# Four graph-attention layers on one core: exponentials and row forms in one pool of six buffers, an 18th weight buffer, and copies of G issued ahead of evictions

## Chip, cores and metric

The kernel runs on one core of a Trainium2 chip. The metric is the device time of one execution in microseconds (us); the kernel before takes 2480.03 us, the median of 3 runs (2478.59 to 2482.91).

The core's engines are named as in the profile: PE multiplies matrices (PEld is its loading of weights, which overlaps), ACT applies functions and copies, DVE and POOL do elementwise work, SP issues most of the transfers (DMA). Each engine runs its instructions in the order in which the program issues them; engines wait for each other by semaphores.

## What is computed

Input `x` holds 16 graphs of 1,024 nodes with 256 features, `adj` one 1,024 x 1,024 adjacency matrix for all. Four attention layers follow each other. Each takes the layer norm of x, then a relu, and adds the attention's result to x. Layers 0 and 2 have 4 heads of 64 features, layers 1 and 3 one head of 256. Cut to one head, a layer is

```python
h = jnp.maximum(_layernorm(x, axis=-1), 0.0)
Wh = jnp.matmul(h, W)
e = leaky(Wh @ a[:D] [:, None] + Wh @ a[D:] [None, :])   # slope 0.2, layer 3: 0.01
alpha = softmax(jnp.where(adj > 0, e, -inf), axis=-1)
x = x + elu(jnp.matmul(alpha, Wh))                       # layer 3: relu
```

## The kernel before

**Steps.** A step is one layer of one graph: 64 steps. Four graphs are in work at a time, and `order_of_steps` interleaves their layers so that from step 8 to step 58 even steps are one-head and odd steps four-head. Each pair of steps takes the same course.

**Preparation of a step** works on two halves of four chunks of 128 nodes. DVE takes the statistics of x (L240), POOL combines them to a shift and a factor (L267 to L279), ACT normalises (L285) into a form called `xn`, ACT splits its 32-bit words into 16-bit halves, `bits` (L294), a DMA transposes these into `turned` (L296), and ACT merges them into the transposed rows `hT` (L302). xn, bits, turned and hT all come from one pool of buffers by the name "rows", HBUFS = 5 of 4 KB a partition. PE projects hT with the layer's matrix, 8 chunks of 2 matmuls (L327); ACT evicts each chunk (L329). From the projection follow, for every node, exponential factors: `rcol` for the sources; those for the targets go through DRAM (L345 to L355) and come back as G, one row of 1,024 values on all partitions, fetched by DMA into `gs` (L371).

**Weights.** For each head ACT copies gs into PSUM (`broadcast`, L383, two buffers: this is "a copy of G"). DVE then makes the head's eight weight tiles, one instruction each (`weights`, L388): max(g, rcol) * mask, 128 x 1,024 values in a buffer of the pool "w", WBUFS = 17. A buffer is free again when the group of matmuls that reads the head's last rows is done.

**Aggregation.** PE multiplies weight tiles with the projected features (L404), and ACT evicts the sums to `y` (L419). A step has eight groups: in a one-head step one block of 128 rows each, so all eight read the same eight tiles; in a four-head step half of a head's rows, so that two groups use up a head.

**Finish.** The step before is finished in pieces during the next step: DVE takes reciprocals (L440), POOL scales y (L450), and for layers 0 to 2 the elu follows: min(y, 0) into a tile `e` (L447 to L452), its exponential on ACT (L456), the sum on DVE (L462), the addition to x on POOL (L463). Layer 3 has a relu and the addition in one DVE instruction (L465). The `e` tiles have two buffers of their own, 4 KB a partition each.

**The order of the instructions** is written out by the loop at the end (L608 to L628). For every group it issues: weight tiles that this group needs and that are still missing; the group's matmuls and its eviction; pieces of the finish that are due; copies of G for the heads that come next (`emit_heads`, L517 to L525); the preparation's pieces due at this group (tables FOUR, ONE and so on, in groups from the step two before); and further weight tiles up to `upto`, the least of six (four-head) or three (one-head) more than issued and of the freed buffers plus WBUFS. `emit_heads(i)` copies a head if its first tile's place is at most

```python
min(i + C // 2, done["tiles"] + C, len(tiles) - 1)        # L519, C = 8
```

and only if its step is prepared. The same function is called by `emit_tiles` (L527) ahead of each tile.

**Weight columns.** The projection matrices of layers 1 to 3 get extra columns, W times the attention vectors, in pieces at fixed groups: the vectors are loaded (L139 on) into a tile of the name "e", spread over the partitions by a matmul (L149), multiplied on DVE into the columns, and bounds for the exponents are taken.

Of the kernel before, what the change touches and what calls it, by code (L numbers as in the profile page):

```python
# [26 lines left out]
F32 = mybir.dt.float32  # L27
# [9 lines left out]
P = 128  # L37
EPS = 1e-5
SHIFT = 60.0
STREAMS = 4  # L40
WBUFS = 17
HBUFS = 5

# [22 lines left out]
def kernel(ctx: ExitStack, tc: tile.TileContext, x, adj, ws, avs, out):  # L68
    nc = tc.nc
    B, N, F = x.shape  # L70
    C = N // P
    K = F // P
    HALF = C // 2
# [26 lines left out]
    prep = ctx.enter_context(tc.tile_pool(name="prep", bufs=2))  # L100
    small = ctx.enter_context(tc.tile_pool(name="small", bufs=4))
    work = ctx.enter_context(tc.tile_pool(name="work", bufs=2))
# [30 lines left out]
    def weight_columns(l):  # L133

        H, slope, hs, _ = LAYERS[l]
        D = F // H
        st = {}

        def vectors(queue=nc.sync):  # L139

            st["a"] = prep.tile([P, HALF, H, D], F32, name="e")
            queue.dma_start(
                out=st["a"][0:1, 2:4],
                in_=bass.AP(tensor=avs[l].tensor, offset=avs[l].offset,
                            ap=[[0, 1], [D, 2], [hs, H], [1, D]]))

        def spread():
            pa = bank(2, H, D)
            nc.tensor.matmul(pa.rearrange("p t h d -> p (t h d)"), lhsT=ones[0:1, :],  # L149
                             rhs=st["a"][0:1, 2:4].rearrange("p t h d -> p (t h d)"),  # L150
                             start=True, stop=True)
            nc.scalar.activation(st["a"][:, 0:2], pa, AF.Copy)

        def columns(ks=range(K)):
            for k in ks:
                for part in range(2):
                    prod = st["a"][:, 2 + part]
                    wk = heads_of(wx[l], H)[:, k]
                    nc.vector.tensor_mul(prod, wk[:, :, 0:D], st["a"][:, part])
                    nc.vector.tensor_reduce(  # L160
                        wk[:, :, D] if part else wx[l][:, k, F + H:F + 2 * H], prod, AX.X, ALU.add)
            if K - 1 not in ks:
                return
            st["sq"] = small.tile([P, K, H], F32, name="sq", bufs=1)
            wd = heads_of(wx[l], H)[:, :, :, D]
            nc.vector.tensor_tensor(st["sq"], wd, wd, op=ALU.mult)

        def bound():

            pn = bank(H)  # L170
            for k in range(K):
                nc.tensor.matmul(pn, lhsT=ones, rhs=st["sq"][:, k, :], start=(k == 0),
                                 stop=(k == K - 1))
            top = small.tile([P, 1], F32, name="top", bufs=1)
            nc.vector.tensor_reduce(top, pn, AX.X, ALU.max)
            nc.gpsimd.tensor_tensor(top, top, half1, op=ALU.pow)
            nc.gpsimd.tensor_scalar(cbias[l], top, 16.01, None, op0=ALU.mult)
            nc.gpsimd.tensor_scalar(nbias[l], top, -16.01 * slope, None, op0=ALU.mult)
            nc.gpsimd.tensor_scalar(rbias[l], top, -16.01 * (1.0 - slope), SHIFT,
                                    op0=ALU.mult, op1=ALU.add)  # L180

        return vectors, spread, columns, bound

    pairs = {}
# [240 lines left out]
    def finish(n):  # L425

        b, l = steps[n]
        H = LAYERS[l][0]
        D = F // H
        st = state[n]  # L430

        def views(half):
            s = slice(half * HALF, (half + 1) * HALF)
            return (xs[b][:, s, :].rearrange("p c (h d) -> p (c h) d", h=H),
                    st["y"][:, s, :, 0:D].rearrange("p c h d -> p (c h) d"),
                    st["r"][:, s, :].rearrange("p c h -> p (c h)"))

        def divide():
            st["r"] = small.tile([P, C, H], F32, name="r")
            nc.vector.reciprocal(st["r"], st["y"][:, :, :, D])  # L440

        def scaled(half):
            xh, yh, r = views(half)
            rb = r[:, :, None].to_broadcast([P, HALF * H, D])
            if l < L - 1:

                e = st["e", half] = prep.tile([P, HALF * H, D], F32, name="e")  # L447
                if H > 1 and slack(n):
                    nc.vector.scalar_tensor_tensor(e, yh, 0.0, rb, op0=ALU.min, op1=ALU.mult)  # L449
            nc.gpsimd.tensor_tensor(yh, yh, rb, op=ALU.mult)  # L450
            if l < L - 1 and not (H > 1 and slack(n)):
                nc.gpsimd.tensor_scalar(e, yh, 0.0, -3.0e38, op0=ALU.min, op1=ALU.max)  # L452

        def exponential(half):
            if l < L - 1:
                nc.scalar.activation(st["e", half], st["e", half], AF.Exp)  # L456

        def add(half):
            xh, yh, r = views(half)
            if l < L - 1:  # L460
                e = st["e", half]
                nc.vector.scalar_tensor_tensor(e, e, -1.0, yh, op0=ALU.add, op1=ALU.max)  # L462
                nc.gpsimd.tensor_add(xh, xh, e)  # L463
                return
            nc.vector.scalar_tensor_tensor(xh, yh, 0.0, xh, op0=ALU.max, op1=ALU.add)  # L465

        def store(half):
            nc.sync.dma_start(
                out=out[b].rearrange("(p c) f -> p c f", p=P)[:, half * HALF:(half + 1) * HALF],
                in_=xs[b][:, half * HALF:(half + 1) * HALF, :])  # L470
            if half == 1 and b + STREAMS < B:
                load(b + STREAMS)


        at = (0, 0, 0, 0, 1, 1, 1) if slack(n) and H > 1 else (0, 0, 1, 1, 2, 2, 3)
        return list(zip(at, (divide, lambda: scaled(0), lambda: scaled(1), lambda: exponential(0),
                             lambda: exponential(1), lambda: add(0), lambda: add(1)))) + (
                    [(4, lambda: store(0)), (4, lambda: store(1))] if l == L - 1 else [])
# [38 lines left out]
    def emit_heads(i):  # L517

        while done["g"] <= min(i + C // 2, done["tiles"] + C, len(tiles) - 1):  # L519
            n, h, _ = tiles[done["g"]]  # L520
            if n >= done["prepared"]:
                break
            broadcast(n, h)
            done["g"] += C
            fetch_heads()  # L525
# [13 lines left out]
    for n, (b, l) in enumerate(steps):  # L539

        free = -99
        if b % STREAMS in last:
            over = last[b % STREAMS] + 1
            free = 8 * over + (8 if l == 0 else 2 if LAYERS[steps[over][1]][0] == 1 else 4)
        last[b % STREAMS] = n
        start = 8 * (n - 2)
        kind = ONE if LAYERS[l][0] == 1 else SOON if n < 5 else FOUR
        if kind is FOUR and free > start + kind[0]:
            kind = SHORT
        if kind is ONE and free > start + kind[0]:  # L550
            kind = TIGHT
        if free > start + kind[0]:
            kind = LATE
            start = max(free, agenda_of[-1][0] + 5, start - LATE[7])
        agenda_of.append([start + k for k in kind] if n > 1 else FIRST)
        if n > 2:

            assert agenda_of[n][7] >= 8 * (n - 2)
            assert agenda_of[n][3] >= agenda_of[n - 1][12]
    ending = []  # L560
    later = {}
    with tc.manual_schedule():
# [40 lines left out]
            load_weights(i)  # L603

        for l, at in ((1, 1), (2, 8 * 3 + 3), (3, 8 * 5 + 3)):
            for i, piece in zip((0, 1, 2, 8), layer[l]):
                later[at + i] = piece
        for n in range(len(steps)):  # L608
            for k, (h, i0, per) in enumerate(groups(n)):
                while planned < len(steps) and min(  # L610
                        a[0] for a in agenda_of[planned:planned + 2]) <= 8 * n + k:
                    plan(planned)
                    planned += 1
                emit_tiles(place[n, h, C - 1] + 1, must=True)
                aggregate(n, h, i0, per)
                if i0 + per == C:
                    done["free"] = place[n, h, C - 1] + 1
                while ending and ending[0][0] <= k:
                    ending.pop(0)[1]()
                upto = min(done["tiles"] + (6 if per > 1 else 3), done["free"] + WBUFS)  # L620
                emit_heads(upto - 1)
                if 8 * n + k in later:
                    later[8 * n + k]()
                prepare(8 * n + k)
                emit_tiles(upto)
            for _, piece in ending:
                piece()
            ending = finish(n) if n < len(steps) - 1 else []  # L628
# [35 lines left out]
```

## Time and profile before

| | before |
|---|---|
| time, median of 3 | 2480.03 us |
| span of the profiled execution | 2479.7 us |
| PE busy | 2403.9 us |
| DVE busy | 2044.1 us |
| ACT busy | 1482.8 us |
| POOL busy | 1071.2 us |
| weight tiles (L388), 1,280 | 1540.8 us, 1274 ns each |
| copies of G (L383), 159 | 162.7 us, 1023 ns each |
| splits (L294), 124 | 236.2 us, 1905 ns each |
| merges (L302), 124 | 265.7 us, 2143 ns each |

The profile is of one execution. A line of the time line has the start, the length, the engine, the line of the kernel, the operation, its output and inputs by the program's names, and in brackets how long the engine was idle before it and what it waited for. In lists of waits the three numbers are the total in us, the number of waits and the longest. The ends of matmuls are modelled.

### The profile page before, as it was taken

The numbers are of one execution on the slowest core, as the hardware profiler recorded it, in microseconds if no ns is written. First come the engines' busy times: TensorE is split into PE (matmuls) and PEld (weight loads), VectorE is DVE, ScalarE is ACT, GpSimd is POOL, SyncE is SP. The second block draws the span as 40 slices with busy tenths as digits, with TensorE's granted clock in tenths as the row PEclk, the third lists the DMA queues.
The fourth block names the chain that finished last, engine by engine and source line by source line (L and its number), as shares of the span: only waits on it lengthen the run. The fifth ranks groups of instructions, "written<-read, shape, count | busy, mean of one in ns | idle before, by whom it ended". The sixth has DMA issues, their size and how long they took to land.

```text
span 2479.7 us, 86492 instructions
## 1 busy us (share of the span) xinstructions
PE 2403.9 (97%) x39104; PEld 2158.6 (87%) x39104; DVE 2044.1 (82%) x2138; ACT 1482.8 (60%) x2501; POOL 1071.2 (43%) x1366
## 2 busy tenths in 40 slices
PE   7899999999999999999999999999999999999989
PEld 5788898898898888888889888889888898888878
DVE  8997677888888988888888888888888888887963
ACT  5465666556665556755556765656655566666451
POOL 3235455443344444544433554543444444554341
PEclk9999999999999999999999999999999999999999
DMA  4322232333433322323433322223334322323221
GB/s 179 80 54 61 44 79 53 78 96 79 112 72 93 79 55 52 79 62 103 109 91 88 79 62 70 70 55 94 95 76 106 104 55 61 79 56 75 72 52 60
DMA packets 294760, 193.39 MB, mean 78 GB/s; under 512 B 264182, under 2 KB 266998, under 8 KB 292472
## 3 DMA queue, kind: packets, MB, share of 16 engines
q1 hardware_dynamic: 294382, 187.86, 30.5%
q8 instruction: 306, 5.01, 0.8%
q14 instruction: 62, 0.51, 0.1%
q10 hardware_dynamic: 10, 0.00, 0.0%
HBM read 105.39 MB, written 17.43 MB: 50 GB/s over the span
## 4 chain that ended last, share of the span: by engine, by line
PE 86%; DVE 6%; DMA 3%; ACT 3%; issue 2%; POOL 1%; DVEq 0%; SPq 0%; ACTq 0%; POOLq 0%
PE bank L404 68%; PE bank L327 17%; DVE w L388 4%; DMA rows<-rows 3%; ACT rows L302 1%; DVE bn L240 1%; ACT rows L285 0%; DVE e L462 0%; ACT rows L294 0%; POOL rstd L273 0%; DVE mask L213 0%; POOL x L463 0%; DMA x<-in_x 0%; PE bank L351 0%; DVE wx L160 0%
## 5 line engine op out<-in xcount | busy, mean ns | idle before, releaser
L404 PE MATMUL bank<-whx,w 128*64 128x65 f32 x36864 | 1909.4, 241 | 40.1 <-DVE w L388 27.5
L404 PEld LDWEIGHTS bank<-whx,w 128*64 128x64 f32 x36864 | 1755.3, 145 | 200.6 <-DVE w L388 33.8
L388 DVE SCALAR_TENSOR_TENSOR w<-g,rcol,mask 128x1024 f32<-128x1024 f32 x1280 | 1540.8, 1274 | 232.6 <-PE bank L404 135.9
L339 POOL TENSOR_TENSOR whx<-whx 128x1024 f32<-128x1024 f32 x128 | 243.4, 1902 | 858.8 <-ACT whx L337 858.8
L419 ACT ACTIVATE y<-bank 128x260 f32<-128x260 f32 (+1 forms) x504 | 191.9, 384 | 658.1 <-PE bank L404 657.8
L327 PE MATMUL bank<-wx,rows 128*128 128x264 f32 (+1 forms) x2048 | 487.3, 392 | 14.5 <-ACT rows L302 7.5
L327 PEld LDWEIGHTS bank<-wx,rows 128*128 128x128 f32 x2048 | 383.6, 192 | 89.4 <-ACT rows L302 15.5
L450 POOL TENSOR_TENSOR y<-y,r 128x1024 f32<-128x1024 f32 x126 | 260.7, 2078 | 233.8 <-DVE e L449 180.5
L463 POOL TENSOR_TENSOR x<-x,e 128x1024 f32<-128x1024 f32 x96 | 227.1, 2365 | 179.8 <-DVE e L462 179.8
L285 ACT ACTIVATE rows<-x,shift,rstd 128x256 f32<-128x256 f32 x512 | 264.6, 589 | 65.6 <-POOL shift L279 64.0
L329 ACT ACTIVATE whx<-bank 128x264 f32<-128x264 f32 (+1 forms) x512 | 189.4, 385 | 170.3 <-PE bank L327 169.9
L302 ACT ACTIVATE rows<-rows 128x2048 uint16<-128x2048 uint16 x124 | 265.7, 2143 | 21.1 <-DMA rows<-rows 21.1
L294 ACT ACTIVATE rows<-rows 128x2048 uint16<-128x2048 uint16 x124 | 236.2, 1905 | 2.2
L462 DVE SCALAR_TENSOR_TENSOR e<-e,y 128x1024 f32<-128x1024 f32 x96 | 190.9, 1989 | 50.1 <-ACT e L456 41.5
L240 DVE BATCH_NORM_STATS2 bn<-x 128x6 f32<-128x256 f32 x512 | 175.5, 410 | 33.2 <-POOL x L463 30.0
L383 ACT ACTIVATE g<-gs 128x1024 f32<-128x1024 f32 x159 | 162.7, 1023 | 27.1 <-DVE w L388 15.1
L273 POOL TENSOR_TENSOR rstd<-rstd,neghalf 128x4 f32<-128x4 f32 (+1 forms) x97 | 120.2, 1239 | 15.0 <-DVE shift L274 7.6
L456 ACT ACTIVATE e<-e 128x1024 f32<-128x1024 f32 x96 | 100.8, 1050 | 1.0 <-POOL e L452 1.0
L440 DVE RECIPROCAL r<-y 128x32 f32<-128x32 f32 (+1 forms) x63 | 17.3, 275 | 82.9 <-ACT y L419 82.8
L449 DVE SCALAR_TENSOR_TENSOR e<-y,r 128x1024 f32<-128x1024 f32 x58 | 68.5, 1222 | 2.1
L465 DVE SCALAR_TENSOR_TENSOR x<-y,x 128x1024 f32<-128x1024 f32 x30 | 36.5, 1218 | 8.9 <-POOL y L450 8.9
L337 ACT ACTIVATE whx<-whx,nbias 128x16 f32<-128x16 f32 (+1 forms) x128 | 40.3, 315 | 4.2
(67 smaller groups left out, 443.6 us busy)
## 6 DMA issues: line engine op xcount, KB each, us to landing
gs<-grow SPq DMA_DIRECT2D x159, 512.0 KB
x<-in_x SPq DMA_DIRECT2D x15, 1024.0 KB
out<-x SPq DMA_DIRECT2D x30, 512.0 KB
w<-in_adj SPq DMA_DIRECT2D x8, 512.0 KB
rows<-rows SPq DMA_TRANSPOSE x124
x<-in_x SPq DMA_DIRECT2D x2, 512.0 KB
wx<-in_L_gnn_W SPq DMA_DIRECT2D x8, 128.0 KB
out<-x SPq DMA_DIRECT2D x8, 128.0 KB
```

The source lines that it names most:

```text
L240: nc.vector.bn_stats(bn[:, c, :], xs[b][:, c, :])
L285: nc.scalar.activation(xn[:, :, q, :], xs[b][:, c, :].rearrange("p (k i) -> p k i", k=K), AF.Relu, bias=st["shift"][:, c:c + 1], scale=st[ ...
L294: nc.scalar.activation(bits, xn.rearrange("p (n s) -> p s n", s=2), AF.Copy)
L302: nc.scalar.activation(st["hT", half].rearrange("p k i -> p (k i)").bitcast(U16).rearrange("p (n s) -> p n s", s=2), st["turned", half].re ...
L327: nc.tensor.matmul(pw, lhsT=st["hT", half][:, k, q * P:(q + 1) * P], rhs=wx[l][:, k, :], start=(k == 0), stop=(k == K - 1))
L339: nc.gpsimd.tensor_tensor(wh[:, :, :, 0:D], wh[:, :, :, 0:D], wh[:, :, :, D:D + 1].to_broadcast([P, HALF, H, D]), op=ALU.mult)
L388: nc.vector.scalar_tensor_tensor(w, state[n]["g", h], state[n]["rcol"][:, jc, h:h + 1], masks[LAYERS[steps[n][1]][3]][:, jc, :], op0=ALU.m ...
L404: nc.tensor.matmul(acc[o % P:o % P + cols, q, :], lhsT=st["w", h, jc][:, o:o + cols], rhs=st["whx"][:, jc, h * (D + 1):(h + 1) * (D + 1)], ...
L419: nc.scalar.activation(st["y"][:, i0:i0 + per, h, :], acc, AF.Copy)
L450: nc.gpsimd.tensor_tensor(yh, yh, rb, op=ALU.mult)
L462: nc.vector.scalar_tensor_tensor(e, e, -1.0, yh, op0=ALU.add, op1=ALU.max)
L463: nc.gpsimd.tensor_add(xh, xh, e)
```

## The change

The change has three parts.

- Buffers. The `e` tiles of the finish come from the pool "rows", which grows from 5 to 6 buffers; the vectors of the weight columns come from the pool "w", which grows from 17 to 18. The two buffers of "e" are gone, so that the memory stays the same.
- The pieces of the weight columns: vectors, then spread and columns together one group later, bounds eight groups after the vectors as before. So the weight buffer that the vectors take is given back sooner.
- Order. The freed buffers and `upto` are worked out ahead of the group's aggregation, and `emit_heads` is called ahead of it too, with C // 2 = 4 more in one-head steps. It is meant to have G ready before DVE wants it, in place of behind the eviction and the pieces of the finish, and a whole head ahead.

```diff
-WBUFS = 17
-HBUFS = 5
+WBUFS = 18
+HBUFS = 6
...
-            st["a"] = prep.tile([P, HALF, H, D], F32, name="e")
+            st["a"] = work.tile([P, HALF, H, D], F32, name="w", bufs=WBUFS)
...
-                e = st["e", half] = prep.tile([P, HALF * H, D], F32, name="e")
+                e = st["e", half] = prep.tile([P, HALF * H, D], F32, name="rows",
+                                                    bufs=HBUFS)
...
-            for i, piece in zip((0, 1, 2, 8), layer[l]):
-                later[at + i] = piece
+            vectors, spread, columns, bound = layer[l]
+            later[at] = vectors
+            later[at + 1] = lambda spread=spread, columns=columns: (spread(), columns())
+            later[at + 8] = bound
...
                 emit_tiles(place[n, h, C - 1] + 1, must=True)
-                aggregate(n, h, i0, per)
                 if i0 + per == C:
                     done["free"] = place[n, h, C - 1] + 1
+                upto = min(done["tiles"] + (6 if per > 1 else 3), done["free"] + WBUFS)
+
+                emit_heads(upto - 1 + (0 if per > 1 else C // 2))
+                aggregate(n, h, i0, per)
                 while ending and ending[0][0] <= k:
                     ending.pop(0)[1]()
-                upto = min(done["tiles"] + (6 if per > 1 else 3), done["free"] + WBUFS)
-                emit_heads(upto - 1)
```

## The prediction

> **What bounds the kernel now.** I began with the busy shares and the chain of work that ended last.
>
> ```profile
> PE 2403.9 (97%) x39104; PEld 2158.6 (87%) x39104; DVE 2044.1 (82%) x2138; ACT 1482.8 (60%) x2501; POOL 1071.2 (43%) x1366
> PE 86%; DVE 6%; DMA 3%; ACT 3%; issue 2%; POOL 1%; DVEq 0%; SPq 0%; ACTq 0%; POOLq 0%
> ```
>
> PE works for 2403.9 of 2479.7 us, so an edit that leaves the matmuls alone can gain at most 75.8 us. The answer by windows says where they lie: PE is idle for 36.8 us before 400, 23.0 us between 400 and 2240 and 16.3 us after. The change touches little of the first and third, so the steady part comes next: the list of waits between 467 and 2260, which are 24 equal pairs of a one-head step (even) and a four-head step (odd), (2260.39 - 467.05) / 24 = 74.7 us each. PE's entries:
>
> ```profile
> PE bank L404 <- issue: 9.3, 9, 1.6
> PE bank L404 <- DVE w L388: 5.3, 24, 0.2
> PE bank L327 <- ACT whx L329: 4.6, 7, 1.2
> PE bank L327 <- issue: 1.1, 2, 0.6
> PE bank L327 <- ACT rows L302: 0.3, 1, 0.3
> ```
>
> Columns are the total, the number, the longest. Only the second is a wait that the change is aimed at: once a pair, 0.22 us, for a weight tile. DVE's own waits for G (L388 <- ACT g L383) are large, 61.2 us in 24, but DVE is not the bound. So I ask not what DVE gains but what the moved copies do to what PE waits for. That needs the time line of ACT in one pair (one-head step 34; columns: start, length, instruction, idle before it and releaser):
>
> ```profile
> 1374.96 0.38 ACT L419 ACTIVATE y<-bank 128x257 f32<-128x257 f32 x1 [2.17 <-PE bank L404]
> 1375.24 1.02 ACT L383 ACTIVATE g<-gs 128x1024 f32<-128x1024 f32 x1
> 1378.09 2.07 ACT L285 ACTIVATE rows<-x,shift,rstd 128x256 f32<-128x256 f32 x4 [1.82 <-POOL shift L279]
> 1380.19 1.91 ACT L294 ACTIVATE rows<-rows 128x2048 uint16<-128x2048 uint16 x1
> 1382.01 0.37 ACT L419 ACTIVATE y<-bank 128x257 f32<-128x257 f32 x1
> 1382.27 2.06 ACT L285 ACTIVATE rows<-x,shift,rstd 128x256 f32<-128x256 f32 x4
> 1384.37 1.91 ACT L294 ACTIVATE rows<-rows 128x2048 uint16<-128x2048 uint16 x1
> 1386.19 0.37 ACT L419 ACTIVATE y<-bank 128x257 f32<-128x257 f32 x1
> 1386.45 2.14 ACT L302 ACTIVATE rows<-rows 128x2048 uint16<-128x2048 uint16 x1
> ```
>
> and PE's beside it:
>
> ```profile
> 1383.67 5.16 PE L404 MATMUL bank<-whx,w 128*128 128x257 f32 x23
> 1388.66 3.51 PE L327 MATMUL bank<-wx,rows 128*128 128x258 f32 x15
> ```
>
> From 1378.09, when POOL's shift releases the first normalisation, to 1388.59, when the first merge (L302) ends, ACT has no gap. The first projection (L327) needs that merge and starts at 1388.66, 0.07 us after it. PE's one-head aggregation, begun at 1364.33 and 24.33 us long, ends at 1388.66 as well. So the merge comes exactly in time, with no slack: whatever is put into this chain of ACT reaches PE in full. The step two earlier shows the same (merge 1312.66 to 1314.79, projection at 1314.87). Twice the trace shows a later merge, once this:
>
> ```profile
> 411.41 2.15 ACT L302 ACTIVATE rows<-rows 128x2048 uint16<-128x2048 uint16 x1 [0.40 <-DMA rows<-rows]
> 413.61 2.67 PE L327 MATMUL bank<-wx,rows 128*128 128x258 f32 x11 [0.43 <-ACT rows L302]
> ```
>
> A merge 0.40 us late cost PE 0.43 us; at 1911.51 one 0.37 us late cost 0.30.
>
> **What the Trainium skill says.** "Perfetto Trace Analysis", in the part on the Tensor Engine's instruction, says that ACT, DVE and GpSimd are strictly first in, first out, and that PE's end times are modelled. The trace agrees on ACT: the eviction at 1386.19 stood behind split and normalisation, though its group had been done some 3.6 us earlier (six groups of 24.33 / 8 = 3.04 us from 1364.33 end at 1382.6). "ScalarE: Activation LUTs", in the part on what ACT_TABLE_LOAD costs, gives an ACTIVATE with immediate scale and bias 186 ns + 0.833 ns a column, 1039 ns for 1,024, and an overlap of about 93 ns with its neighbour. The trace has 1.02 us for a copy of G, and 0.95 us to the next start in a full queue (255.38 to 256.32 is 0.94). I take 0.95 us.
>
> **The change, part by part.**
>
> *Copies of G ahead of evictions, a head ahead.* I followed the loop by hand for the pair above, counting weight tiles. Step 35's tiles begin at place p; at step 34's sixth group (k=5) nine of them have been issued, and the new bound is min(upto - 1 + 4 + 4, tiles + 8) = p + 17, so that head 2's copy (place p + 16) is emitted there, before that group's eviction. In the kernel before, head 2's copy follows the first eviction of step 35 (1396.61). In the ACT queue it now stands between the second split and the eviction at 1386.19, in the middle of the full chain. Behind it: that eviction, the first merge, two more evictions; behind the merge: PE's first projection. Its own inputs are no wait: its PSUM buffer is head 0's, whose eighth tile DVE ends at about 1385.6 (1375.94 + 8 x 1.2), before the split ends at 1386.28. Head 1's copy stays in the gap before 1378.09 (it moves ahead of the eviction at 1374.96, which waits 2.17 us anyway), so it buys the chain nothing. The merge, and with it PE, is 0.95 us later in each pair with an even step from 10 to 56: 24 x 0.95 = +22.8. Step 8 has 0.4 us of slack: +0.55. Steps 3 and 6 have 3.3 and 1.6: nothing.
>
> What it gives: DVE's wait for head 2's copy, 2.51 us before 1397.66, goes. But DVE's next tile waits 4.13 us, until 1403.08, for a weight buffer that PE frees, so the earlier tile only lengthens that wait. Gain on PE: nothing.
>
> *The 18th buffer.* DVE may run one tile further ahead. In the four-head step head 2's eighth tile, now behind the elu at 1410.23 (or L465 for the relu layers), goes ahead of it, and the 0.22 us that PE waits for it at 1412.70 disappears: 25 x 0.22 = -5.5.
>
> *Prologue and tail.* Step 4 stalls 3.46 us at 257.64 because the statistics (L240, 2.7 us) stand before a tile; with another buffer they stand after it: -2.7. The same reordering delays preparation of steps 3 and 4 by a tile (1.2): +1.2. Among the last steps one stall shrinks by a tile, -1.2, and one preparation comes a tile later, +1.2. Together -1.5.
>
> *Columns.* The column vector's tile moves to the pool of weight buffers and its pieces together. It happens three times, and the slot is given back before the first group that would want it: 0, at most 1.2 each.
>
> *The pool of six.* Two exponential tiles and five forms share six buffers. In relu layers no exponential exists, and the sixth buffer is free. In the pairs with an elu one-head layer the second split at 1411.80 finds live: two exponentials (POOL adds them from 1411.54 to 1413.92 and from 1415.08 to 1417.47), first bits, first turned, second rows, and itself: exactly six. So whether anything waits depends on which buffer a tile gets. The compiled kernel before takes the longest free one, not the next in rotation (one merge takes the buffer of four requests ago, the next preparation that of six), so I take no wait: 0. The other end is the split waiting for the POOL add, 2.1 us, in 13 pairs.
>
> Sum: +22.8 + 0.55 - 5.5 - 1.5 = +16.4. From 2480.0: **2496 us**.
>
> **Rivals.**
>
> *The pool waits as well.* If buffers came in strict rotation, the second split would want the first exponential's buffer, and wait from 1411.80 to 1413.92; transpose, merge and second half of the projection follow, and the next first merge would wait for the second exponential. I work out 0.4 to 2.15 us in each of 13 pairs, 1.5 in the mean, 19.5 together: 2515.9. For it: exactly six are live. Against: the buffers of before do not rotate.
>
> *The copy is hidden.* If the order of ACT does not turn out as counted, or the chain moves earlier because POOL's shift does, only the gains stand: 2480.0 - 5.5 - 1.5 = 2473, or 2470 if gaps called issue shrink too. For it: ACT is busy only 60%, and the shift depends on DVE, which has fewer waits. Against: the statistics before the shift wait for POOL (1374.62, 1.16 <- POOL x L463), which the change doesn't speed up, and the chain is full in every pair that I looked at.
>
> *No change.* Half of the delay is absorbed somewhere: 11.7 - 5.5 - 1.5 = +4.7, 2484.7, which can't be told from no change. Nothing in the trace speaks for exactly that.
>
> **How the numbers follow.** Copy in the chain alone 0.60 (0.85 to 1.02 us a copy, columns 0 to 3.6, prologue and tail -2.5 to 0: 2493 to 2503), with pool waits too 0.17 (to 2518), hidden 0.13 (2468 to 2475), in balance 0.10. The range from 2478 to 2518 leaves out the hidden case and the far ends. Faster 0.13, same 0.10, slower 0.77.
>
> **What would show it.** DVE's waits for ACT g L383 should nearly vanish (61.2 us before) and PE's 0.22 us waits for w L388 too. PE or its weight loads should wait about 0.95 us before the first projection of each one-head step for rows L302, some 23 us together, with a G copy between split and merge in ACT's time line; the pair grows to about 75.4 us. A wait of split or merge for POOL x L463 would show the first rival. I am wrong if the first merge still ends with the aggregation: then the chain began earlier, or the copy stands elsewhere.

## The result, and the profile after

The changed kernel takes 2500.3 us (median of 4 runs, 2499.28 to 2502.73): 1.0089 times the kernel before, 95% interval 1.0067 to 1.011. The forecast was 2496. The profiled execution is 2498.4 us long, 18.7 us more than before. Its busy shares and its chain of work that ended last:

```profile
PE 2404.9 (96%) x39104; PEld 2152.7 (86%) x39104; DVE 2043.2 (82%) x2138; ACT 1483.5 (59%) x2501; POOL 1072.8 (43%) x1366
PE 67%; DVE 11%; ACT 10%; DMA 5%; issue 5%; POOL 2%; DVEq 0%; ACTq 0%; POOLq 0%
```

No engine has more work: PE is busy for 2404.9 us, 2403.9 before. But the chain now runs through ACT for 10% of the span, 3% before. The time is idle time of PE, and the list of PE's waits between 467 and 2260 names it (total, number, longest):

```profile
PE bank L327 <- ACT rows L302: 19.3, 24, 0.9
PE bank L404 <- issue: 8.6, 8, 1.7
PE bank L327 <- ACT whx L329: 5.9, 12, 1.6
PE bank L327 <- issue: 0.8, 2, 0.5
PE bank L327 <- ACT y L419: 0.2, 1, 0.2
```

The first line stood at 0.3 us in one wait before; now it comes once in each of the 24 pairs. The wait for a weight tile (L404 <- DVE w L388, 5.3 us before) is gone. The time line of ACT in the one-head step that answers to the one shown of before:

```profile
1382.55 2.07 ACT L285 ACTIVATE rows<-x,shift,rstd 128x256 f32<-128x256 f32 x4 [2.75 <-POOL shift L279]
1384.65 1.91 ACT L294 ACTIVATE rows<-rows 128x2048 uint16<-128x2048 uint16 x1
1386.47 0.37 ACT L419 ACTIVATE y<-bank 128x257 f32<-128x257 f32 x1
1386.74 2.06 ACT L285 ACTIVATE rows<-x,shift,rstd 128x256 f32<-128x256 f32 x4
1388.83 1.91 ACT L294 ACTIVATE rows<-rows 128x2048 uint16<-128x2048 uint16 x1
1390.65 1.01 ACT L383 ACTIVATE g<-gs 128x1024 f32<-128x1024 f32 x1
1391.59 0.37 ACT L419 ACTIVATE y<-bank 128x257 f32<-128x257 f32 x1
1391.86 2.13 ACT L302 ACTIVATE rows<-rows 128x2048 uint16<-128x2048 uint16 x1
```

and PE's:

```profile
1385.73 7.55 PE L404 MATMUL bank<-whx,w 128*128 128x257 f32 x34
1394.04 3.75 PE L327 MATMUL bank<-wx,rows 128*128 128x258 f32 x16 [0.76 <-ACT rows L302]
```

The copy of G (L383) has come to lie between the second split and the sixth eviction, and the merge ends 0.94 us later after the first normalisation than before (11.44 us in place of 10.50). The normalisation itself starts equally late in both kernels: 13.76 us after PE resumes the aggregation behind the transpose of the factors (L351) in the same step (1378.09 - 1364.33; 1382.55 - 1368.79). So nothing made up for the copy. PE's true loss is larger than the 0.76 us in brackets, since that wait is counted from a modelled end of the last matmul. The distance between starts is safer: from that resumption, the first matmul of the step's second group, to the first projection it is 24.39 us in the mean of 24 steps before, and 25.30 us after. This distance, called A below, turned out to be the sharpest reading of all.

DVE no longer waits for G (61.2 us before), but

```profile
DVE w L388 <- PE bank L404: 155.9, 24, 6.6
```

its wait for a freed weight buffer rose from 99.0 to 155.9 us: the sum of both is 160.2 before and 155.9 after.

Three readings locate the 18.7 us: +0.5 up to the first projection of step 12 (491.27 before, 491.79 after), +14.1 in the 23 pairs from there (74.74 to 75.35 us a pair), +4.1 from the last of these projections to the end (269.4 to 273.5 us). The +0.5 is a sum of larger parts; "The start" below takes it apart.

### The profile page after: what moved, and what is told of

It reads as the page before. It is cut to its first block, busy times and chain, and to the rows that moved or that the text cites. A ratio compares the mean times of both kernels' runs of the same rounds, so it can differ in the third digit from the quotient of the medians.

```text
span 2498.4 us, 86573 instructions
## 1 busy us (share of the span) xinstructions
PE 2404.9 (96%) x39104; PEld 2152.7 (86%) x39104; DVE 2043.2 (82%) x2138; ACT 1483.5 (59%) x2501; POOL 1072.8 (43%) x1366
## 4 chain that ended last, share of the span: by engine, by line
PE 67%; DVE 11%; ACT 10%; DMA 5%; issue 5%; POOL 2%; DVEq 0%; ACTq 0%; POOLq 0%
PE bank L404 50%; PE bank L327 17%; DVE w L388 8%; DMA rows<-rows 4%; ACT rows L302 4%; ACT rows L285 2%; DVE rows L463 2%; POOL x L464 1%; DVE bn L240 1%; ACT g L383 1%; ACT y L419 1%; ACT rows L457 1%; PE bank L351 0%; ACT rows L294 0%; POOL rstd L273 0%
## 5 line engine op out<-in xcount | busy, mean ns | idle before, releaser
L404 PE MATMUL bank<-whx,w 128*64 128x65 f32 x36864 | 1902.5, 241 | 32.2 <-DVE w L388 19.3
L404 PEld LDWEIGHTS bank<-whx,w 128*64 128x64 f32 x36864 | 1749.3, 145 | 191.5 <-issue 28.1
L388 DVE SCALAR_TENSOR_TENSOR w<-g,rcol,mask 128x1024 f32<-128x1024 f32 x1280 | 1537.9, 1272 | 215.1 <-PE bank L404 187.1
L419 ACT ACTIVATE y<-bank 128x260 f32<-128x260 f32 (+1 forms) x504 | 189.9, 383 | 598.7 <-PE bank L404 596.7
L329 ACT ACTIVATE whx<-bank 128x264 f32<-128x264 f32 (+1 forms) x512 | 188.9, 386 | 195.8 <-PE bank L327 195.2
L464 POOL TENSOR_TENSOR x<-x,rows 128x1024 f32<-128x1024 f32 x96 | 227.2, 2367 | 179.6 <-DVE rows L463 179.6
L302 ACT ACTIVATE rows<-rows 128x2048 uint16<-128x2048 uint16 x124 | 265.6, 2142 | 20.9 <-DMA rows<-rows 20.8
L463 DVE SCALAR_TENSOR_TENSOR rows<-rows,y 128x1024 f32<-128x1024 f32 x96 | 192.1, 2002 | 45.5 <-ACT rows L457 38.3
L383 ACT ACTIVATE g<-gs 128x1024 f32<-128x1024 f32 x159 | 161.8, 1019 | 47.9 <-DVE w L388 24.7
L457 ACT ACTIVATE rows<-rows 128x1024 f32<-128x1024 f32 x96 | 100.6, 1048 | 0.1
L450 DVE SCALAR_TENSOR_TENSOR rows<-y,r 128x1024 f32<-128x1024 f32 x58 | 70.1, 1251 | 2.1
```

Source lines behind the costliest of these rows:

```text
L302: nc.scalar.activation(st["hT", half].rearrange("p k i -> p (k i)").bitcast(U16).rearrange("p (n s) -> p n s", s=2), st["turned", half].re ...
L388: nc.vector.scalar_tensor_tensor(w, state[n]["g", h], state[n]["rcol"][:, jc, h:h + 1], masks[LAYERS[steps[n][1]][3]][:, jc, :], op0=ALU.m ...
L404: nc.tensor.matmul(acc[o % P:o % P + cols, q, :], lhsT=st["w", h, jc][:, o:o + cols], rhs=st["whx"][:, jc, h * (D + 1):(h + 1) * (D + 1)], ...
L419: nc.scalar.activation(st["y"][:, i0:i0 + per, h, :], acc, AF.Copy)
```

## The experiments

All in one table. A is the distance just named, "pair" the mean of 23 pairs, "end" the stretch from the last of them to the end; these three are from one profile each, and the time is the median, with the ratio to the kernel before and its 95% interval. How far one profile can be trusted shows in e11, whose steady part has the same instructions as the changed kernel's: its pair takes 75.47 us, 75.35 there.

| kernel | us | ratio (interval) | A | pair | end |
|---|---|---|---|---|---|
| before | 2478 to 2482 | | 24.39 | 74.74 | 269.4 |
| changed | 2500.3 | 1.0089 (1.0067 to 1.011) | 25.30 | 75.35 | 273.5 |
| e1 buffers alone | 2481.7 | 1.0 (0.999 to 1.0011) | 24.40 | 74.75 | 269.6 |
| e2 order alone | 2505.1 | 1.0097 (1.008 to 1.0114) | 25.32 | 75.55 | 273.6 |
| e3 copy behind the merge | 2474.5 | 0.9971 (0.9962 to 0.9981) | 24.42 | 74.67 | 269.5 |
| e4 no head further ahead | 2474.2 | 0.9979 (0.9971 to 0.9987) | 24.40 | 74.63 | 270.0 |
| e5 idle copy, sixth group | 2501.5 | 1.0089 (1.0076 to 1.0103) | 25.29 | 75.84 | 268.3 |
| e6 idle copy, fourth group | 2479.1 | 1.0002 (0.9995 to 1.001) | 24.38 | 74.75 | 268.9 |
| e7 e3, split sooner | 2538.9 | 1.0239 (1.0214 to 1.0264) | 24.42 | 77.02 | 271.3 |
| e8 merge ahead of the copy | 2488.1 | 1.0033 (1.0022 to 1.0045) | 24.41 | 74.99 | 273.9 |
| e9 before, no second transpose | 2470.4 | 0.9969 (0.9958 to 0.9981) | 24.41 | 74.50 | 268.5 |
| e10 e1, no second transpose | 2462.5 | 0.9935 (0.9923 to 0.9947) | 24.37 | 74.17 | 267.4 |
| e11 changed, step 58 as e4 | 2499.8 | 1.0069 (1.0046 to 1.0092) | 25.30 | 75.47 | 269.2 |

**The two halves of the change.** e1 keeps the buffers and undoes the order:

```diff
-                emit_heads(upto - 1 + (0 if per > 1 else C // 2))
                 aggregate(n, h, i0, per)
...
+                emit_heads(upto - 1)
```

> The changed kernel with the order of the loop as before: 18 weight buffers, the pool of six and the columns' new places are kept, the copies of G stand behind evictions again. Theory (the copy of head 2 lies in a full stretch of ACT that ends in the merge PE waits for): head 2's copy goes behind the last eviction of the one-head step, the first merge ends with the aggregation again, PE's 24 waits of 0.22 us for a weight tile stay away: 2479.3 - 5.5, with prologue and tail between 2470 and 2478. Rival 1 (the pool of six or the 18th buffer costs the time): about 2495 to 2500, as the changed kernel. Rival 3 (a copy ahead of an eviction costs by holding back the eviction's PSUM bank): 2470 to 2478 as well.

e2 is the kernel before with the new order alone.

> The kernel before with the order of the loop alone: 17 weight buffers, five row forms and two exponentials of their own. Theory: head 2's copy stands between the second split and the first merge as in the changed kernel; PE waits 0.8 us for the merge in 24 pairs and keeps the 0.22 us waits: 2479.3 + 19.4, with a few us of the tail: 2498 to 2506. Rival 1: 2476 to 2482. Rival 3: 2498 to 2506.

The split is clean on the main question: A is 25.32 with the order and 24.40 with the buffers, so in the steady part the pool of six and the 18th buffer cost nothing and the order costs all. But e1's time missed the expectation of the theory. It equals the kernel before, although the 0.22 us waits are gone. PE's waits in e1 between 467 and 2260:

```profile
PE bank L404 <- issue: 12.3, 8, 2.5
PE bank L327 <- ACT whx L329: 10.7, 11, 1.7
PE bank L327 <- issue: 0.7, 1, 0.7
```

Waits for the eviction L329 were 4.6 us before and are 10.7 here. This is taken up again in e7, e9 and e10.

**The place of the copy.** e3 is the changed kernel with head 2's copy one group later, behind the merge:

```diff
-                emit_heads(upto - 1 + (0 if per > 1 else C // 2))
+                emit_heads(upto - 1 + (0 if per > 1 or k == 5 else C // 2))
```

> The changed kernel, but at the sixth group of a one-head step heads are copied no further than upto - 1, so that head 2's copy is issued one group later, behind the first merge and ahead of the seventh group's eviction. Theory: PE's waits for the merge vanish, the 0.22 us waits stay away, 2470 to 2479 (the tail may keep up to 4 us of the change). Rival 1: 2495 to 2500. Rival 3: the seventh eviction is held back as the sixth was; 2490 or more.

e4 leaves out C // 2 altogether; head 2's copy is then issued at the eighth group, still ahead of that eviction.

> The changed kernel without the extra C // 2: copies stand ahead of evictions, but no head further ahead; head 2's copy is issued ahead of the eighth group's eviction, behind the first merge. Theory: 2470 to 2479. Rival 1: 2495 to 2500. Rival 3: 2490 or more, with PE waiting for banks in the first projection.

Both fell inside the theory's expectation. The same copy, with the same buffers, is worth 26 us between its places: 2500.3 between split and merge, 2474.5 just behind the merge. A is back at 24.42 and 24.40. In the profiles (2498.4 and 2472.5 us) 15.8 us of the difference lie in the 23 pairs, 4.0 in the end and 6.1 in the start. e3 and e4 are also below the kernel before, by 0.29% and 0.21%; their pairs are only 0.07 and 0.11 us shorter, no more than the changed kernel and e11 differ, so where this gain lies is not shown.

**A copy that nobody needs.** To separate ACT's time from all that an earlier G could do to DVE, e5 adds to the kernel before

```diff
+                if per == 1 and k == 5 and 10 <= n <= 56:
+                    nc.scalar.activation(idle, masks[0][:, 0, :], AF.Copy)
                 aggregate(n, h, i0, per)
```

> The kernel before with one more copy of 1,024 values on ACT (a mask, 8 bits, into a tile that nobody reads) ahead of the sixth group's eviction in the 24 one-head steps from 10 to 56; no buffer, no order and no dependence is changed. Theory (ACT is full from the first normalisation to the first merge, and PE waits for the merge): about 0.9 us a step, 24 x 0.9 = +21.6, 2497 to 2505. Rival (the loss in the changed kernel comes from DVE starting head 2 sooner, or from its memory traffic): 2478 to 2484.

and e6 the same with `k == 3`.

> The same additional copy two groups sooner, ahead of the fourth group's eviction, where ACT waits for PE and then for POOL's shift. Theory: the gap takes it up, 2478 to 2484. Rival (any further instruction in ACT's queue costs, by the evictions behind it): as much as in the sixth group, about 2500.

e5's time line of ACT (line numbers behind the insertions are moved by one or more; L303 is the merge):

```profile
1393.86 1.91 ACT L295 ACTIVATE rows<-rows 128x2048 uint16<-128x2048 uint16 x1
1395.68 1.04 ACT L617 ACTIVATE idle<-mask 128x1024 uint8<-128x1024 uint8 x1
1396.62 0.37 ACT L420 ACTIVATE y<-bank 128x257 f32<-128x257 f32 x1
1396.89 2.14 ACT L303 ACTIVATE rows<-rows 128x2048 uint16<-128x2048 uint16 x1
```

and its first wait of PE:

```profile
PE bank L328 <- ACT rows L303: 19.3, 24, 0.9
```

The idle copy reproduces the changed kernel's wait to the tenth: 19.3 us in 24, A 25.29. It costs 22.9 us in all, 0.95 us each. (In the profile the pair grew by 1.10 us, 0.90 of it in A; the cause of the other 0.20 is not shown.) Two groups earlier, where ACT waits for PE and then for POOL, the same 1.05 us cost nothing (A 24.38). So it is ACT's time in this stretch, and neither DVE's earlier start nor a buffer.

**The merge ahead of the copy.** e8 keeps the copy a head ahead and moves the merge in front of it by due times:

```diff
-ONE = (2, 2, 2, 3, 4, 3, 5, 7, 7, 7, 7, 4, 7, 8, 8, 8, 8, 8, 11, 11, 12)
+ONE = (2, 2, 2, 3, 3.7, 3, 3.9, 7, 7, 7, 7, 3.8, 7, 8, 8, 8, 8, 8, 11, 11, 12)
```

> The changed kernel with the first merge of the one-head steps issued behind the second split of the same group, so ahead of head 2's copy and of the sixth eviction; the copy stays a whole head ahead and ahead of that eviction. Theory (only the place of the copy before the merge costs): 2470 to 2479. Rival (the copy's place before evictions or its earliness costs): 2490 to 2500.

It came out between the two: A is repaired (24.41), and yet a pair takes 0.32 us more than in e3. PE's time line and the list of its weight loads' waits say why:

```profile
1386.58 4.09 PE L327 MATMUL bank<-wx,rows 128*128 128x258 f32 x16
```

```profile
PEld bank L327 <- ACT y L419: 12.3, 25, 0.7
```

The projection's first half takes 4.09 us in place of 3.75: three evictions now stand behind merge and copy together, and the projection runs out of PSUM buffers until they are done. In e3 that line is 0.2 us in one wait. So the third theory, an eviction held back, was not wrong but small: 0.3 us a pair in e8; in the changed kernel, where that line is 0.7 us in one wait, the wait for the merge comes first and hides it.

**Where the gain of the 18th buffer went.** In e1, PE's waits for L329 lie in four-head steps. One of them is seen from ACT:

```profile
1272.61 2.15 ACT L302 ACTIVATE rows<-rows 128x2048 uint16<-128x2048 uint16 x1 [2.54 <-DMA rows<-rows]
1274.66 1.21 ACT L329 ACTIVATE whx<-bank 128x264 f32<-128x264 f32 x4
```

The second half's merge waits 2.54 us for its transpose, and four evictions of the projection stand behind it. In the same pair of the kernel before the merge did not wait; PE had lost 1.15 us to a gap called issue just before. Over all pairs merges waited 22.3 us for transposes in 18 waits in e1, and 16.1 us in 16 before. e7 tried to bring that transpose forward, by splitting one group sooner:

```diff
-FOUR = (-8, -8, -5, 0, 2, 1, 4, 5, 5, 5, 5, 3, 4.5, 5, 5, 5, 5, 6, 8, 8, 10)
+FOUR = (-8, -8, -5, 0, 2, 1, 4, 5, 5, 5, 5, 2, 4.5, 5, 5, 5, 5, 6, 8, 8, 10)
```

> The kernel with head 2's copy behind the first merge (2474.5), and the second split of the four-head steps due at 2 in place of 3, behind the second normalisation and ahead of that group's eviction and of gT, where ACT was idle 1.4 us. Theory (the gain of the 18th buffer was eaten up because the second merge of the four-head step then waits for its transpose, with evictions of the projection behind it): the transpose is issued about 1.8 us sooner, PE's waits for L329 (7.6 us) go, 2466 to 2471. Rival (what PE loses is gaps called issue, and these take the place of any wait that goes; or the fetch of G, now behind the transpose on SP, comes too late): 2472 to 2480.

A miss by far, 64 us above e3. The transposes did come in time: merges waited for them 0.6 us in one wait, in e3 21.1 us in 20. But the rival that the fetch of G comes too late had the direction, though not the size. SP's queue and ACT's answer in one pair:

```profile
1358.97 2.87 SPq L296 DMA_TRANSPOSE rows<-rows  x1
1361.89 0.47 SPq L355 DMA_DIRECT2D grow<-gT  x1
1363.39 0.33 SPq L371 DMA_DIRECT2D gs<-grow  x1
```

```profile
1367.79 1.03 ACT L383 ACTIVATE g<-gs 128x1024 f32<-128x1024 f32 x1 [2.87 <-DMA gs<-grow]
```

Issuing the transpose holds SP until 1361.84, and only then are the next step's factors, on hand since 1359.37, written and fetched. The fetch is issued 5.1 us after PE's transpose of the factors (L351 at 1358.28), 1.9 us in the pair of the kernel before (1262.24 to 1264.15). The copy of G then waits on ACT with evictions behind it, 95.2 us in 39 such waits (5.4 in 8 before), and PE waits for evictions: 24.0 us for L329 and 22.4 us for L419.

So the wait was taken away in another manner. e9 and e10 leave the second transpose of four-head steps out, from the kernel before and from e1:

```diff
+            if half == 1 and H > 1 and n > 8:
+                st["turned", half] = bits.rearrange("p s (n i) -> p s n i", i=P)
+                return
```

> The kernel before, but in four-head steps from the ninth on the second half's transpose by DMA is left out: the merge reads the split's output itself (so the rows of that half are not turned, and the output is not the reference's; every other instruction stays). Theory (in a pair PE either loses about 1 us to a gap called issue or to the eviction L329 that stands behind a merge waiting for its transpose): the merges of this half no longer wait, PE's waits for L329 (4.6 us) go, the 0.22 us waits for tiles stay: 2472 to 2478. Rival (gaps or other waits take their place): 2478 to 2483.

> The same left out of the kernel with the buffers alone (2481.7), where PE waited 10.7 us for L329. Theory: those waits go, and now the 18th buffer shows its gain: 5 us below the same cut in the kernel before, 2467 to 2473. Rival (the 18th buffer is worth nothing because issue gaps take the place of any wait): the same time as the cut in the kernel before, within 2 us.

PE's waits in e9 and in e10 (L407 is the aggregation, L330 the projection):

```profile
PE bank L407 <- issue: 9.8, 6, 2.1
PE bank L407 <- DVE w L391: 5.3, 24, 0.2
PE bank L330 <- ACT rows L305: 0.7, 1, 0.7
PE bank L330 <- issue: 0.4, 1, 0.4
```

```profile
PE bank L407 <- issue: 10.4, 8, 2.4
PE bank L330 <- issue: 1.0, 1, 1.0
PE bank L330 <- ACT rows L305: 0.4, 1, 0.4
PE bank L330 <- ACT whx L332: 0.2, 1, 0.2
```

Without that transpose the waits for the eviction are gone (0 and 0.2 us), the gaps called issue stay about the same, and the 18th buffer shows its gain: 2470.4 against 2462.5, and 0.33 us a pair. Both are some us lower than expected. With the transpose in place the same buffers gave nothing (e1). Leaving it out also frees SP and DMA engines for everything else, so how much of the drop of both belongs to the merge's wait alone stays open; the difference between the two, which share it, does not depend on that. (e10 also has the pool of six and the new places of the columns; it is the vanished L407 <- DVE w line, 5.3 us, that points to the 18th buffer.)

**The end.** In step 58 the changed kernel's copy was not ready to run:

```profile
2295.58 1.03 ACT L383 ACTIVATE g<-gs 128x1024 f32<-128x1024 f32 x1 [3.58 <-DVE w L388]
2296.54 0.37 ACT L419 ACTIVATE y<-bank 128x257 f32<-128x257 f32 x1
2296.80 2.13 ACT L302 ACTIVATE rows<-rows 128x2048 uint16<-128x2048 uint16 x1
```

```profile
2296.96 1.16 PE L327 MATMUL bank<-wx,rows 128*128 128x264 f32 x4 [1.27 <-ACT y L419]
2299.27 5.07 PE L327 MATMUL bank<-wx,rows 128*128 128x264 f32 x14 [1.15 <-ACT whx L329]
```

Its PSUM buffer was still being read by DVE, so it held ACT for 3.58 us, and the eviction and the merge behind it; PE lost 1.27 + 1.15 us there. e11 takes C // 2 away in step 58 alone.

> The changed kernel, with the extra C // 2 left out in step 58 alone, where head 2's copy waits 3.58 us for DVE to free its PSUM buffer, with an eviction and the second merge behind it. Theory: the steady part stays (75.35 us a pair), the stretch from the last pair's first projection to the end, 273.5 us in the changed kernel and 269.4 before, comes back to 269 to 271; the whole 2500.3 - 4 = 2496. Rival (the end is longer because of what the steady part leaves behind): 273 to 274 and 2500.

The end fell to 269.2 us, as in the kernel before, while A stayed at 25.30. The whole time, 2499.8, does not show these 4 us beyond its interval; its profile is longer elsewhere, by 0.12 us a pair and 1.8 us in the start, where the edit changes nothing. What e11 shows rests on the stretch in its profile. The same 273.6 and 273.9 appear in e2 and e8, the other kernels that issue this copy ahead of the sixth group's eviction.

**The start.** In steps 3 and 6 the changed kernel's copy was not ready either. It stood between the second split and the merge and waited for DVE:

```profile
217.76 1.03 ACT L383 ACTIVATE g<-gs 128x1024 f32<-128x1024 f32 x1 [2.00 <-DVE w L388]
335.63 1.03 ACT L383 ACTIVATE g<-gs 128x1024 f32<-128x1024 f32 x1 [2.37 <-DVE w L388]
```

PE then waited 1.96 and 1.40 us for the merges behind these copies. In e1 and e3, whose copies come behind the merge, it waited for neither.

A second loss comes from the pieces of the weight columns. Their first round on DVE, before and after:

```profile
68.59 0.42 DVE L159 TENSOR_TENSOR e<-wx,e 128x256 f32<-128x256 f32 x1
```

```profile
65.36 0.42 DVE L159 TENSOR_TENSOR w<-wx,w 128x256 f32<-128x256 f32 x1 [2.49 <-ACT w L152]
70.04 0.34 PE L404 MATMUL bank<-whx,w 128*64 128x65 f32 x4 [2.54 <-DVE w L388]
```

With spread and columns in one group, the columns stand on DVE ahead of tiles that they stood behind before, and DVE waits for the spread vectors (L152). PE waited for no tile between 57 and 80 us before; now it waits for four there, 4.8 us together. At the first projection of a one-head layer it is 5.6 us late (142.55 for 137.00); in e1, which has the new places of the columns, 4.5 us (141.52), in e2, which has the old ones, not at all (137.05). The columns were not tried alone, so what the rest of the 5.6 us is stays open.

That the start still came out at +0.5 is in part chance. Step 4 gave back 2.9 us, as forecast. But in the profile of before PE also ran at a lower granted clock (the share of full speed that the profile shows): 0.77 from 160 to 175 us and 0.87 from 205 to 218, in the stretches of the changed kernel that answer to these 0.88 (166 to 180) and 1.00 (208 to 221). e5, e6 and e9, whose instructions in most of the start are those of the kernel before, reach the first projection of step 12 at 487.3, 488.8 and 486.7 us, before at 491.3.

## Why the prediction was right, point by point

- **Copies ahead of evictions, +22.8.** Right. Measured: A grew by 0.91 us in 24 pairs, 21.8 us, and the added wait is for L302 as named. The idle copy of e5 gives the same without any other part of the change.
- **Step 8, and no loss in steps 3 and 6.** Steps 3 and 6 are wrong. The slack of 3.3 and 1.6 us was read rightly, but there the copy also brings a wait of its own (2.00 and 2.37 us), and PE waited 1.96 and 1.40 us. Step 8's wait went from 0.43 to 1.10 us, near the 0.55 given; but with the copy behind the merge it is 0.85 in e1 and 1.08 in e3, so that agreement is luck.
- **Step 4, -2.7.** Right: its waits for tiles between 244 and 258 fell from 6.3 to 3.4 us, by 2.9; in e1 they are 3.4 us as well.
- **The 18th buffer, -5.5.** The 0.22 us waits went, as forecast; what that gained is less sure. The rest of the pair (pair less A) fell in the changed kernel from 50.35 to 50.05 us, 0.30 where I had 0.22. But it is 50.23 in e2, with the order alone and 17 buffers, and 50.17 in e11, with 18; so the buffer's part is 0.06 to 0.18, no clearer than one profile against another. In e1, without the new order, it is 50.35 again. I treated the 0.22 us wait as if PE had nothing next to it; the second merge's transpose is due within about a microsecond of the same place and takes over. e9 and e10 show that the buffer gains, 0.33 us a pair, once this is out of the way. Why some of the gain stayed in the changed kernel and none in e1 is only argued: a pair that is 0.9 us longer elsewhere leaves the transpose more time. PE's waits for L329 were 5.9 us there and 1.8 in e2, but 10.7 in e1.
- **Tail, 0 net.** Wrong by 4 us. The step that failed is "Its own inputs are no wait": true in the pair that I looked at, false in step 58, where DVE is later, as in steps 3 and 6. e11 shows it for step 58.
- **Pool of six, 0; columns, 0.** Right for the pool: no wait of ACT for POOL's addition appears in the list between 467 and 2260, and e1's pair equals that of the kernel before. Wrong for the columns, "at most 1.2 each": the first round alone cost PE 4.8 us of waiting. I had asked only when their slot comes free, and not what DVE does behind them.
- **DVE's wait for G buys nothing.** Right: 61.2 us went into the wait for freed buffers.
- **The copy is hidden (0.13).** Fell: POOL's shift came at 13.76 us in both kernels, so the stretch could not begin sooner.
- **A reading that was off.** I took 1364.33 for the start of step 34's aggregation and divided 24.33 us by eight groups. But L351 splits the aggregation, and seven groups follow it, 3.48 us each. The sixth was done at 1381.7, and its eviction at 1386.19 came 4.5 us later, not 3.6. The argument, that it stood behind split and normalisation, stays.

In sum: forecast +16.4; in the profile +0.5 + 14.1 + 4.1 = +18.7. For the 23 pairs alone the forecast was 23 x (0.95 - 0.22) = 16.8, measured 14.1. The mechanism of the pairs is the one forecast. That the whole came so near owes something to luck: losses that were put at nothing (columns, steps 3 and 6, the end) stand against a larger drop in the pair than forecast, step 4, and a lower clock in the start of the profile of before.

The Trainium skill, "Perfetto Trace Analysis", on the Tensor Engine's instruction, calls ACT strictly first in, first out, and this carried the forecast. The trace agrees, and steps 3, 6 and 58 show a harder consequence: an instruction put ahead in a full stretch of such a queue costs about its own length if it is ready (0.91 us here), and holds up what stands behind it for its own wait as well if it is not (2.00, 2.37 and 3.58 us).

## What to carry to other kernels

Before moving an instruction forward in an engine's queue, mark the stretches in which that engine has no gap up to something that the bounding engine needs; inside such a stretch every microsecond counts in full (0.95 us a copy), two groups sooner nothing (e6), even on an engine that is busy 60% of the time. Ask then, at every place where it will stand and not in one pair alone, whether the moved instruction's own inputs and buffers are ready. An engine that only produces for a full set of buffers gains nothing from earlier inputs: its wait changes its name. And a wait of 0.2 us on the bounding engine is worth its length only if no other arrival is due within the same margin; take the neighbour away in an experiment to see it.

## What the runs showed of the hardware

- An ACT copy of 1,024 values a partition from 8 bits to 8 bits took 1.04 us (e5's idle copy, within SBUF), one from 32 to 32 bits 1.02 us (a copy of G, into PSUM): the smaller width gave nothing here.
- Issuing one transpose by DMA holds SP's queue for long: 2.0 us in the median of 124 before, 5.3 at most. A small transfer behind it, 4 KB of factors, was issued 2.5 us after its data were ready in e7 (1361.89 for 1359.37), and the fetch of G behind that 3.2 us later than before.
- A projection short of PSUM buffers shows as a longer group of matmuls (4.09 for 3.75 us) and as a wait of the weight loads, 12.3 us in 25; PE's own list of waits shows 0.3 us of it. And a wait counted from the modelled end of a matmul, 0.76 us, stood for a loss of 0.91. Distances between starts told both.
- The granted clock of a short stretch can differ between executions of the same instructions: 0.77 in the kernel before from 160 to 175 us, where eight matmul records of a projection took 3.89 us, and 1.00 in e5, where they took 2.05.
